# Two graph layers on one core: the products with W1 by Strassen's scheme on pairs of row tiles, and a first stage with B11 turned from PSUM and eleven slots for x

## The chip, the cores and the metric

The kernel runs on one core of one Trainium2 chip. The metric is the device time of one execution, in microseconds (us). Before the change it is 2218.14 us, the median of three runs (2216.73 to 2218.79). The profile is one execution of 2218.9 us.

## The reference, cut to what matters

`x` has 3327 rows of 512, `adj` is 3327 x 3327, all float32.

```python
h = relu(layernorm(x))
q, k, v = h @ Wq.T + bq, h @ Wk.T + bk, h @ Wv.T + bv
a = q @ k.T / sqrt(512) + adj + adj
x = x + softmax(a) @ v

h = relu(layernorm(x))
A2 = adj + eye
dscale = diagonal(A2) ** -0.5
temp = A2 @ h @ W1.T
x = x + relu((dscale[:, None] * A2 * dscale[None, :]) @ temp)
```

The product that is changed is the one with `W1.T`: the rows of `A2 @ h`, 26 tiles of 128 rows, each 128 x 512, times a 512 x 512 matrix, each row then scaled by `dscale`.

## The kernel before

**Stages.** A first stage (lines 269 to 377) merges Wq and Wk into one matrix M, normalizes and turns the 26 row tiles of x, and multiplies them with M. The score stage (lines 382 to 566) makes the exponentials of all scores. Then three large products follow one another, g = 0, 1, 2: the softmax weights times h, A2 times the new h, and A2 times temp. All are in float32, and all use Strassen's scheme in a form with seven products, twice nested in the large ones.

**The three large products.** `steps` (line 933) lists 294 steps: for each g, for each outer product r in `ORDER` (p5, p1, p6, p7, p2, p3, p4), for each of two column strips s (448 and 384 columns per matmul), the steps t = 0 to 5 and a short one, t None. A step loads its left tile three steps ahead and adds up its four block sums on VectorE two steps ahead (`sums`, `four_sums`, lines 171 to 175, 760 to 766). A full step is seven matmuls into seven PSUM banks (lines 779 and 780); a short one is four (line 772). At the end of t = 5, `Gather.first` (lines 804 to 812) takes the first four banks into SBUF, one copy on ScalarE and four operations on VectorE. After the short step, `Gather.rest` (lines 824 to 828) takes the other four and `Gather.settle` (lines 830 to 841) adds the result to the regions `ct` that need it. The right-hand block of a later step is built by `Right.make` (lines 737 to 749; lines 746 and 179 to 182 for p4), which is called three steps before the first strip's step t, so during the last steps of the strip before and the first ones of its own.

**Rows between the steps.** As soon as regions of `ct` are complete, their row tiles go through a 512 x 512 weight: Wv after g = 0 (`attend`), W1 after g = 1 (`temp`, lines 896 to 901), one tile after each full step from step (g = 1, p3, second strip, t = 2) on, into g = 2's p5. `times_weights` (lines 868 to 873) does four matmuls of 512 columns into one PSUM bank that the steps don't use; ScalarE scales the rows by `sd` (dscale) on the way out (line 900), and the tile is stored for g = 2.

**What sets the order.** The large products stand inside `in_order` (lines 122 to 136): each of the five engines runs its instructions in the order in which the program lists them. That order is `run(k)` (lines 1010 to 1037): the loads of step k + 3, the matmuls of step k, `rest` if the step is short, the sums of step k + 2, `first` if t = 5, `settle` if the step is short, then what is listed between the steps (`make`, loads, row tiles). The first stage stands outside `in_order`: there the framework orders each engine's queue. A tile framework inserts the waits between engines and keeps a buffer from being overwritten before its readers are done. `x_ring` (line 269) has seven buffers for x tiles. Lines 307 to 312 take M's blocks out of PSUM, form differences of them (`four_differences`, lines 177 to 182), and turn the sign of the first, B11, in place.

Of the kernel before, what the change touches and what calls it, by code (L numbers as in the profile page):

```python
# [10 lines left out]
F32 = mybir.dt.float32  # L11
AF = mybir.ActivationFunctionType
ALU = mybir.AluOpType
AX = mybir.AxisListType

P = 128
# [20 lines left out]
PAIRS = 6  # L37
# [6 lines left out]
ROW = tuple(STRIPS[s] + y * HT[s] + k for y in range(2) for s in range(2) for k in range(HT[s]))  # L44
# [3 lines left out]
def graph_layers_kernel(  # L48
# [28 lines left out]
    nc = tc.nc  # L77
    N = out.shape[0]
    NP, D = x.shape
    DC = D // P  # L80
    NT = NP // P
    scale = 1.0 / math.sqrt(D)
    E = D // 2
# [16 lines left out]
    def large(k, shape, name):  # L100
        return arena.tile(shape, F32, name=name, tag=f"large{k}")

    def mid(k, shape, name):
        return arena.tile(shape, F32, name=name, tag=f"mid{k}")

    def half(k, shape, name):
        return arena.tile(shape, F32, name=name, tag=f"half{k}")

    def bank(k, name):
        return banks.tile([P, BW], F32, name=name, tag=f"bank{k}")  # L110

    def ring(*slots):

        turn = itertools.cycle(slots)

        def take(shape, name):
            kind, k = next(turn)
            return kind(k, shape, name)

        return take  # L120
# [17 lines left out]
    const = ctx.enter_context(tc.tile_pool(name="const", bufs=1))  # L138
# [29 lines left out]
    rowd = [[dram.tile([P, D], F32, name=f"row{g}_{i}") for i in range(NT)] for g in range(3)]  # L168
# [5 lines left out]
        nc.vector.tensor_add(o[:, 2], o[:, 1], g[:, 0])  # L174
        nc.vector.tensor_add(o[:, 3], o[:, 2], g[:, 2])  # L175

    def four_differences(b):

        yield nc.vector.tensor_sub(b[4], b[0], b[1])
        yield nc.vector.tensor_add(b[5], b[3], b[4])  # L180
        yield nc.vector.tensor_sub(b[6], b[1], b[3])
        yield nc.vector.tensor_sub(b[7], b[2], b[5])
# [32 lines left out]
    B = {"m1": 0, "p2": 2, "p3": 3, "p5": 4, "p6": 5, "p7": 6, "p4": 7}  # L215
# [14 lines left out]
    class Chain:  # L230
# [7 lines left out]
        def __init__(self, product, first, more, last):  # L238


            X, Y, Z = x_bank("X"), y_bank("Y"), z_bank("Z")
            product(Y, "m1", True)
            first(0, Y, -1)
            product(Z, "p5", True)
            first(3, Z, -1)
            product(X, "p2", True)
            more(0, X)
            product(Y, "p6", False)
            first(1, Y, -1)
            Chain.finish()  # L250
            product(Z, "p3", False)
            more(1, Z)
            product(Y, "p7", False)
            more(3, Y)

            def rest():
                product(Y, "p4", False)
                first(2, Y, 1)
                last()

            Chain.before = rest
# [4 lines left out]
                Chain.before()  # L266
            Chain.before = None

    x_ring = ring(*((mid, k) for k in range(10, 15)), (half, 13), (half, 14))
    n_ring = ring(*((mid, k) for k in range(4)))  # L270

    def load_x(i, queue=nc.sync):
# [6 lines left out]
    def blocks(slots, name):  # L279

        return [b[:, k] for b in (half(j, [P, 2, 2, E], name) for j in slots) for k in range(2)]
# [3 lines left out]
    first = {}  # L285
# [7 lines left out]
    M = blocks(range(4, 8), "M")  # L293
# [8 lines left out]
    ps = [bank(k, "mm") for k in range(DC)]  # L302
    for c in range(DC):
        for r in range(DC):
            nc.tensor.matmul(ps[r], w_q[c // 2][:, c % 2, r * P : (r + 1) * P], w_k[c // 2][:, c % 2],
                             start=c == 0, stop=c == DC - 1)
    for r in range(DC):
        for z in range(2):
            nc.scalar.mul(M[2 * (r // 2) + z][:, r % 2], ps[r][:, z * E : (z + 1) * E], scale)
    for _ in four_differences(M):  # L310
        pass
    nc.scalar.mul(M[0], M[0], -1.0)

    def h_transposed(k):

# [53 lines left out]
    for r in range(DC):  # L369
        for c in range(DC):  # L370
            nc.tensor.matmul(pu[:, r : r + 1], w_k[c // 2][:, c % 2, r * P : (r + 1) * P], bq_sb[:, c : c + 1],
                             start=c == 0, stop=c == DC - 1)
# [144 lines left out]
    steps = [(n, t) for n in range(len(groups)) for t in range(HALF)]  # L517
# [32 lines left out]
    with in_order(*(e.engine for e in (nc.vector, nc.tensor, nc.gpsimd, nc.sync))):  # L550
# [9 lines left out]
        k = len(steps)  # L560
# [16 lines left out]
    ROLE = {"p1": 0, "p6": 2, "p7": 4, "p5": 6, "p2": 7, "p3": 1, "p4": 5, "p8": 3}  # L577
# [35 lines left out]
    sd = const.tile([P, NT], F32, name="sd")  # L613
    rs = const.tile([P, NT], F32, name="rs")

    def weights(src):

        w = [half(k, [P, 2, D], "w") for k in (12, 13)]
        for c in range(DC):
            nc.sync.dma_start(w[c // 2][:, c % 2], src[c * P : (c + 1) * P])  # L620
        return [w[c // 2][:, c % 2] for c in range(DC)]
# [14 lines left out]
    def prepared():  # L636
        nc.vector.reciprocal(rs, tot)
        nc.vector.tensor_scalar(dg, dg, 1.0, None, op0=ALU.add)
        nc.gpsimd.tensor_tensor(sd, dg, mh, op=ALU.pow)

    wv_w1 = []

    def other_weights():
        wv_w1.append(weights(w1T))


    parts = {}
# [1 line left out]
    def view(k, j):  # L649
        if k not in parts:  # L650
            n = PACKS[k][1]
            parts[k] = large(k, [P, n, 4, Q[0]], f"part{k}")
        return parts[k][:, j]
# [9 lines left out]
    cts = {}  # L663
# [9 lines left out]
    spare = [(mid, k) for k in range(10, 15)]  # L673
# [1 line left out]
    x_slots = [lambda k=k: view(2, 1).rearrange("p a w -> p (a w)")[:, k * D : (k + 1) * D] for k in range(3)]  # L675
    x_slots = itertools.cycle([*x_slots, lambda: mid(10, [P, D], "xt")])
    h_ring = ring((mid, 11))
    ts_ring = ring(*spare[:3])
    xr_ring = ring(*spare[:3], (half, 14))
    out_ring = ring((half, 12), (half, 13), *spare[3:])  # L680
    xr_last = ring(*((half, k) for k in (4, 5, 6)))
# [23 lines left out]
    class Right:  # L705
# [9 lines left out]
        def rows(self, dst, h, z):  # L715

            for k, i in enumerate(self.its):
                src = rowd[self.g][ROW[h * HALF + i]]
                nc.sync.dma_start(dst[:, k], src if z is None else src[:, z * E : (z + 1) * E])
# [31 lines left out]
    class Step:  # L751
# [8 lines left out]
        def sums(self):  # L760
            for a, d in self.diagonals:
                nc.vector.tensor_add(a, a, d)
            if self.t is None:
                return
            self.o = o_ring3()[:, :, : Q[self.s]]
            four_sums(self.o, self.a.rearrange("p k y w -> p (k y) w"))
# [76 lines left out]
    def where(i):  # L843

        s = int(i >= STRIPS[1])
        return (s, *divmod(i - STRIPS[s], HT[s]))
# [21 lines left out]
    def times_weights(i, w):  # L868
        s, y, k = where(i)
        ps = bank(ROLE["p8"], "p8")  # L870
        for d in range(DC):
            nc.tensor.matmul(ps, cts[s][y][d][:, k * P : (k + 1) * P], w[d], start=d == 0, stop=d == DC - 1)  # L872
        return ps
# [19 lines left out]

    normed = {}

    def temp(i):

        ps = times_weights(i, wv_w1[1])
        ts = ts_ring([P, D], "ts")
        nc.scalar.mul(ts, ps, sd[:, i : i + 1])  # L900
        nc.gpsimd.dma_start(rowd[2][i], ts)

    xrs = {}

# [28 lines left out]
    steps = [Step(g, r, s, t, rights[g, r, t]) for g in range(3) for r in ORDER for s in range(2) for t in every]  # L933
# [3 lines left out]
    def number_of(g, r, s, t):  # L937
        return ((g * len(ORDER) + r) * 2 + s) * len(every) + t

    def at(k, what, *args):  # L940
        between.setdefault(k, []).append((what, args))

    early = []
    for g in range(3):
        for n, r in enumerate(ORDER):
            for t, e in enumerate(every):
                k = number_of(g, n, 0, t)
# [9 lines left out]
    for n, job in enumerate(jobs):  # L957
        k = k0 + n * (k1 - k0) // len(jobs)
# [3 lines left out]
    def rows(g, k, i, *z):  # L962

        if g == 0:
            at(k - 2, attend_load, i)
            at(k, attend, i)
            at(k + 1, attended, i)
        elif g == 1:
            at(k, temp, i)
        else:  # L970
            at(k - 1, finish_load, i, *z)
            at(k, finish, i, *z)

    for g in range(2):
        k = number_of(g, 5, 1, 2)
        for i in ROW:
            if steps[k].t is None:
                k += 1  # L980
            rows(g, k, i)
            k += 1
    within = {}
    for (n, s, t), its in {
        (5, 1, 2): (0,), (5, 1, 3): (1,), (5, 1, 4): (2,), (5, 1, 5): (3,),
# [3 lines left out]
        for i, when in zip(its, (between, within)):  # L989
            if i is not None:  # L990
                k = number_of(2, n, s, t)
# [5 lines left out]
        at(number_of(2, 6, 1, 2) + n, last_load, i)  # L997
    for k, what in ((1, totals), (2, prepare), (6, prepared), (8, judge), (9, judged)):
        at(k, what)
    at(number_of(1, 1, 0, 4), other_weights)  # L1000

    for k in range(3):
        steps[k].load()
# [4 lines left out]
    banks_of, gathers = {}, {}  # L1008

    def run(k):  # L1010
        step = steps[k]
        if k + 3 < len(steps):
            steps[k + 3].load()
        if step.t == 0:
            banks_of.update(seven())
        if not cts:
            set_up()
        if step.t is None:
            banks_of["p8"] = bank(ROLE["p1"], "p8")
        t, sums = step.t, steps[k + 2].sums if k + 2 < len(steps) else tuple  # L1020
        if t == PAIRS - 1:
            gathers[step.r, step.s] = Gather(step.r, step.s, k == len(steps) - 2)
        gatherer = gathers.get((step.r, step.s))
        for j, _ in enumerate(step.multiply(banks_of)):
            if j == 3 and t == PAIRS - 1 and gatherer.last:
                gatherer.first(banks_of)
            for what, args in within.get(k, ()) if j == 3 else ():
                what(*args)
        if t is None:
            gatherer.rest(banks_of)  # L1030
        sums()
        if t == PAIRS - 1 and not gatherer.last:
            gatherer.first(banks_of)
        if t is None:
            gatherer.settle()
        for what, args in between.get(k, ()):
            what(*args)

    with in_order(*(e.engine for e in (nc.vector, nc.tensor, nc.gpsimd, nc.scalar, nc.sync))):
        for k in range(len(steps)):  # L1040
# [379 lines left out]
```

## Time and profile before

| | before |
|---|---|
| time, median of 3 | 2218.14 us |
| TensorE busy | 2181.7 us, 98% of the span |
| VectorE busy | 1628.5 us, 73% |
| ScalarE busy | 231.5 us, 10% |
| matmuls with Wv and W1 (L872) | 416 records of 512 columns, 123.5 and 65.7 us busy |

A row of the groups reads: line, engine, operation, output<-inputs by the program's names, shapes, count, then busy time and mean duration of one in ns, then the idle time of the engine before them and what ended it. A float32 matmul appears as two records. Durations of matmuls overlap, since they are pipelined; the distance between two starts is the time that one costs. In a list in order of time the columns are start, duration, engine, line, operation, and in brackets the idle time before it with its releaser. In a table of windows they are the window, its length, the busy time of PE, PEld (weight loads), DVE (VectorE), ACT (ScalarE) and POOL with counts, the mean granted clock of TensorE (1.00 is full), the busy share of the DMA engines, and GB/s. In several groups the name `part` stands for different views of the same large buffers, `ct` and the block sums `o` among them.

### The profile page before, as it was taken

To read this page: it belongs to the slowest core of one execution; us is meant where nothing else is said; L and a number is where in the kernel's file an instruction comes from. 1 tells how busy PE (TensorE), PEld (TensorE's weight loads), DVE (VectorE), ACT (ScalarE), POOL (GpSimd) and SP (SyncE) were. 2 spreads that over 40 slices of the span, in tenths; PEclk is the share of its full clock that TensorE was granted. 3 is DMA by queue.
4 is the path that set the end of the run, shared out by engine and by line. 5 is a ranking of instruction groups with operands and counts; after the bars stand their busy time and mean duration, and the time that the engine had idled before them with its cause. 6 is when DMAs were issued, how large, how long until landed. Compare 5 with 4: busy or idle time off the path is not lost.

```text
span 2218.9 us, 20976 instructions
## 1 busy us (share of the span) xinstructions
PE 2181.7 (98%) x6268; PEld 1169.2 (53%) x6268; DVE 1628.5 (73%) x3103; ACT 231.5 (10%) x336; POOL 356.1 (16%) x551
## 2 busy tenths in 40 slices
PE   9999999999999999999999999999999999999997
PEld 6555555455545555555454555555545555555554
DVE  6369888888877788787778778886645358777776
ACT  5312112112110000000001000000000000000011
POOL 4224333333331000001222100000000000000001
PEclk9999999999999999999999999999999999999999
DMA  7558888888969898888797899876645458765685
GB/s 252 211 206 296 292 304 281 301 286 309 348 198 322 310 371 309 273 297 298 261 314 258 303 340 355 283 277 199 225 142 179 135 188 294 248 194 183 206 303 171
DMA packets 246682, 583.68 MB, mean 263 GB/s; under 512 B 34768, under 2 KB 106270, under 8 KB 246558
## 3 DMA queue, kind: packets, MB, share of 16 engines
q1 hardware_dynamic: 192270, 399.28, 54.2%
q0 software_dynamic: 44928, 167.49, 19.9%
q10 hardware_dynamic: 9360, 15.47, 2.1%
q8 instruction: 52, 0.85, 0.2%
q14 instruction: 72, 0.59, 0.1%
HBM read 414.28 MB, written 167.85 MB: 262 GB/s over the span
## 4 chain that ended last, share of the span: by engine, by line
PE 81%; issue 6%; DMA 4%; DVE 4%; POOL 3%; ACT 0%; SPq 0%; POOLq 0%; ACTq 0%; DVEq 0%
PE p L780 52%; PE Y L452 9%; PE p L872 8%; PE p L772 5%; PE Z L452 4%; PE X L452 2%; DMA g<-in_adjT_dram 1%; DMA xt<-in_x_dram 1%; PE Y L345 1%; DVE part L173 1%; DMA xr<-x1d 1%; DMA p<-g 0%; POOL sum L444 0%; PE pt L925 0%; POOL p L460 0%
## 5 line engine op out<-in xcount | busy, mean ns | idle before, releaser
L780 PE MATMUL p<-part,b 128*128 128x448 f32 (+1 forms) x3528 | 1255.4, 514 | 6.1 <-DVE part L174 4.9
L780 PEld LDWEIGHTS p<-part,b 128*128 128x128 f32 x3528 | 669.2, 190 | 571.8 <-issue 309.9
L173 DVE TENSOR_TENSOR part<-part 128x896 f32<-128x896 f32 (+1 forms) x252 | 257.1, 1020 | 95.8 <-PE p L780 50.6
L452 PE MATMUL Y<-qt,hp 128*128 128x448 f32 (+1 forms) x832 | 311.1, 516 | 4.9 <-DVE g L456 3.8
L452 PEld LDWEIGHTS Y<-qt,hp 128*128 128x128 f32 x832 | 157.8, 191 | 142.2 <-issue 73.8
L452 PE MATMUL Z<-qt,hp 128*128 128x384 f32 (+1 forms) x416 | 162.5, 513 | 0.0
L175 DVE TENSOR_TENSOR part<-part,part 128x448 f32<-128x448 f32 (+1 forms) x219 | 129.5, 591 | 16.6 <-DVE part L174 0.5
L174 DVE TENSOR_TENSOR part<-part,part 128x448 f32<-128x448 f32 (+1 forms) x219 | 129.5, 591 | 7.4
L772 PE MATMUL p<-part,b 128*128 128x448 f32 (+1 forms) x336 | 124.2, 513 | 0.0
L872 PE MATMUL p<-w,ct 128*128 128x512 f32 x272 | 123.5, 593 | 0.5 <-DVE part L884 0.5
L452 PEld LDWEIGHTS Z<-qt,hp 128*128 128x128 f32 x416 | 78.8, 190 | 67.4 <-issue 37.2
L456 DVE SCALAR_TENSOR_TENSOR g<-g,Y 128x384 f32<-128x384 f32 (+1 forms) x156 | 91.4, 586 | 29.0 <-PE Y L452 26.3
L866 POOL DMA_DIRECT2D sum<-job x52 | 28.4, 547 | 504.1 <-DVE job L863 285.5
L809 DVE TENSOR_TENSOR part<-p,part 128x384 f32<-128x384 f32 (+1 forms) x33 | 19.4, 586 | 106.5 <-PE p L780 105.9
L772 PEld LDWEIGHTS p<-part,b 128*128 128x128 f32 x336 | 63.6, 190 | 53.7 <-issue 32.3
L808 ACT COPY part<-p 128x384 f32<-128x384 f32 (+1 forms) x33 | 16.6, 503 | 685.4 <-PE p L780 684.6
L872 PEld LDWEIGHTS p<-w,ct 128*128 128x128 f32 x272 | 51.5, 190 | 59.8 <-issue 51.9
L452 PE MATMUL X<-qt,hp 128*128 128x384 f32 (+1 forms) x208 | 81.1, 512 | 0.0
L459 ACT ACTIVATE g<-g 128x768 f32<-128x768 f32 (+1 forms) x48 | 43.0, 896 | 357.3 <-DVE g L456 293.1
L444 POOL DMA_DIRECT2D sum<-o x52 | 36.8, 709 | 224.9 <-DVE o L438 154.1
L872 PE MATMUL p<-w,part 128*128 128x512 f32 x144 | 65.7, 592 | 0.0
L92 POOL DMA_DIRECT2D out_dram<-r x30 | 16.2, 542 | 303.9 <-DVE r L928 268.8
(166 smaller groups left out, 1881.5 us busy)
## 6 DMA issues: line engine op xcount, KB each, us to landing
part<-sum SPq DMA_DIRECT2D x104, 448.0 KB, 5.0
part<-p SPq DMA_DIRECT2D x91, 448.0 KB, 6.5
part<-sum SPq DMA_DIRECT2D x104, 384.0 KB, 3.5
part<-p SPq DMA_DIRECT2D x91, 384.0 KB, 4.1
part<-in_adjT_dram SPq DMA_DIRECT2D x78, 448.0 KB, 4.6
b<-row SPq DMA_DIRECT2D x234, 128.0 KB, 4.9
part<-in_adjT_dram SPq DMA_DIRECT2D x78, 384.0 KB, 3.7
g<-in_adjT_dram SPq DMA_DIRECT2D x52, 448.0 KB, 4.5
```

What stands on the lines that cost most here:

```text
L173: nc.vector.tensor_add(o[:, 0:2], g[:, 0:4:3], g[:, 1:2].to_broadcast([P, 2, g.shape[-1]]))
L174: nc.vector.tensor_add(o[:, 2], o[:, 1], g[:, 0])
L175: nc.vector.tensor_add(o[:, 3], o[:, 2], g[:, 2])
L345: nc.tensor.matmul(ps[:, :w], M[B[name]][:, c, o * P : (o + 1) * P], hp[k][:, A[name], c], start=start and c == 0, stop=c == 1, skip_group ...
L444: nc.gpsimd.dma_start(self.to(sumd)[:, 0:2], self.o)
L452: nc.tensor.matmul(ps[:, :wd], h_of(self.t, name, k), qt[B[name]][:, k], start=start and k == 0, stop=k == 1, skip_group_check=True)
L456: nc.vector.scalar_tensor_tensor(a[n], a[n], 2.0, ps[:, :wd], op0=ALU.mult, op1=ALU.add if sign > 0 else ALU.subtract)
L459: nc.scalar.activation(g[1], g[1], AF.Exp, **({"bias": pad} if self.t == HALF - 1 else {}))
L772: yield nc.tensor.matmul(ps[("p2", "p3", "p4", "p8")[k]][:, :w], b[:, z], a[:, 0, y], start=k == 3, stop=True)
L780: yield nc.tensor.matmul(ps[r][:, :w], b[:, i], m, start=self.t == 0, stop=self.t == PAIRS - 1 and r in ("p1", "p5", "p6", "p7"))
L866: nc.gpsimd.dma_start(sumd[self.s][self.j][:, 2 + self.k], self.a)
L872: nc.tensor.matmul(ps, cts[s][y][d][:, k * P : (k + 1) * P], w[d], start=d == 0, stop=d == DC - 1)
```

## The change

**W1.** A pair of row tiles, each 128 x 512, is taken as a 2 x 2 block matrix: its blocks are the two halves of each tile along the 512 that is summed over. W1 is loaded as four blocks of 256 x 256, and four differences of them are formed ahead, in the second stage. One pair then takes seven products, each of two matmuls with 256 columns, in place of eight block products. VectorE forms four block sums of the pair's rows (eight additions of 128 x 128) at the end of the step before; the seven products are set among the matmuls of two steps, two matmuls apart. They share one PSUM bank, in two halves. Four products leave PSUM through ScalarE, three through VectorE, which adds them to what is there. The scaling by `sd`, or by its negative `nsd`, is done on the way. In these steps the sums of step k + 2 are listed after the second matmul, and not after the last.

**First stage.** M's first block leaves PSUM with its sign turned, and the first difference is formed from the turned block in one operation; the separate turning goes. Nine buffers of one kind and two of another hold x tiles, eleven in place of seven.

The diff, cut:

```diff
-    def four_differences(b):
-        yield nc.vector.tensor_sub(b[4], b[0], b[1])
+    def four_differences(b, first=0):
+        if first == 0:
+            yield nc.vector.tensor_sub(b[4], b[0], b[1])
...
-    x_ring = ring(*((mid, k) for k in range(10, 15)), (half, 13), (half, 14))
+    x_ring = ring(*((mid, k) for k in range(6, 15)), (half, 13), (half, 14))
...
-            nc.scalar.mul(M[2 * (r // 2) + z][:, r % 2], ps[r][:, z * E : (z + 1) * E], scale)
-    for _ in four_differences(M):
+            turned = -scale if r < 2 and z == 0 else scale
+            nc.scalar.mul(M[2 * (r // 2) + z][:, r % 2], ps[r][:, z * E : (z + 1) * E], turned)
+    nc.vector.scalar_tensor_tensor(M[4], M[0], -1.0, M[1], op0=ALU.mult, op1=ALU.subtract)
+    for _ in four_differences(M, 1):
         pass
-    nc.scalar.mul(M[0], M[0], -1.0)
...
+        nc.scalar.mul(nsd, sd, -1.0)
...
-    def temp(i):
-        ps = times_weights(i, wv_w1[1])
-        ts = ts_ring([P, D], "ts")
-        nc.scalar.mul(ts, ps, sd[:, i : i + 1])
-        nc.gpsimd.dma_start(rowd[2][i], ts)
+    PARTS = (("p2", 1, True, 0, 1), ("m1", 0, True, 0, -1), ("p5", 1, False, 3, -1), ("p6", 0, False, 1, -1),
+             ("p3", 1, False, 1, 1), ("p7", 0, False, 3, 1), ("p4", 0, False, 2, 1))
+    AFTER = ((0, 0), (0, 2), (0, 4), (0, 6), (1, 1), (1, 3), (1, 5))
+    class Temp:
...
+        def sums(self):
+            a11, a12, a21, a22 = self.blocks = [
+                [cts[s][y][2 * z + c][:, k * P : (k + 1) * P] for c in range(2)]
+                for s, y, k in map(where, self.its) for z in range(2)
+            ]
+            self.o = half(14, [P, 4, 2, P], "rows")
+            for k, x, y in ((1, a21, a22), (2, None, a11), (3, None, a12), (0, a11, a21)):
+                for c in range(2):
+                    nc.vector.tensor_add(self.o[:, k, c], self.o[:, {2: 1, 3: 2}[k], c] if x is None else x[c], y[c])
+        def product(self, j):
+            name, h, new, n, sign = PARTS[j]
+            if j == 0:
+                self.ps = bank(ROLE["p8"], "pw").rearrange("p (k e) -> p k e", k=2)
+                self.to = [next(ts_slots)() for _ in self.its]
+            left, ps = {"m1": 0, "p2": 1, "p4": 3}.get(name), self.ps[:, h]
+            for c in range(2):
+                a = self.o[:, {"p7": 0, "p5": 1, "p6": 2, "p3": 3}[name], c] if left is None else self.blocks[left][c]
+                nc.tensor.matmul(ps, a, W[B[name]][:, c], start=new and c == 0, stop=c == 1, skip_group_check=True)
+            i = self.its[n // 2]
+            to, by = self.to[n // 2][:, n % 2 * E : (n % 2 + 1) * E], (sd if sign > 0 else nsd)[:, i : i + 1]
+            if name in ("p2", "p5", "p6", "p4"):
+                nc.scalar.mul(to, ps, by)
+            else:
+                nc.vector.scalar_tensor_tensor(to, ps, by, to, op0=ALU.mult, op1=ALU.add)
+            if j == len(PARTS) - 1:
+                for i, ts in zip(self.its, self.to):
+                    nc.gpsimd.dma_start(rowd[2][i], ts)
...
+    k = number_of(1, 5, 1, 2)
+    for n in range(0, NT, 2):
+        if steps[k].t is None:
+            k += 1
+        w = Temp(*ROW[n : n + 2])
+        last_of[k - 1] = w.sums
+        for j, (later, m) in enumerate(AFTER):
+            inserted.setdefault((k + later, m), []).append((w, j))
+        k += 2
...
+        weighs = any((k, j) in inserted for j in range(7))
+        for j, _ in enumerate(itertools.chain((None,), step.multiply(banks_of))):
+            for w, n in inserted.get((k, j), ()):
+                w.product(n)
...
+            if weighs and j == 2:
+                sums()
         if t is None:
             gatherer.rest(banks_of)
-        sums()
+        if not weighs:
+            sums()
         if t == PAIRS - 1 and not gatherer.last:
             gatherer.first(banks_of)
         if t is None:
             gatherer.settle()
         for what, args in between.get(k, ()):
             what(*args)
+        if k in last_of:
+            last_of[k]()
```

## The prediction

> **What bounds the kernel now.** I read first the shares of busy time and the costliest groups.
>
> ```profile
> PE 2181.7 (98%) x6268; PEld 1169.2 (53%) x6268; DVE 1628.5 (73%) x3103; ACT 231.5 (10%) x336; POOL 356.1 (16%) x551
> ...
> L872 PE MATMUL p<-w,ct 128*128 128x512 f32 x272 | 123.5, 593 | 0.5 <-DVE part L884 0.5
> ```
>
> TensorE is the bound: 98% busy, so time leaves only with matmul columns or with its few idle microseconds, and each new wait of TensorE is paid in full. Next, the stage with the W1 products, as one window (PE, PEld, DVE, ACT, POOL, clock, DMA):
>
> ```profile
> 1560.00:1800.00 240.00, 240.00 (x646) 122.38 (x646) 113.03 (x215) 20.23 (x31) 14.03 (x26) 1.00 0.55 172
> ```
>
> Here TensorE never waits, and VectorE is busy 113 of 240 us. An average hides bursts, so I read the order of time across one change of strip, TensorE first:
>
> ```profile
> 1584.31 4.68 PE L780 MATMUL p<-part,b 128*128 128x384 f32 x14
> 1588.83 3.60 PE L872 MATMUL p<-w,ct 128*128 128x512 f32 x8
> 1592.26 2.74 PE L772 MATMUL p<-part,b 128*128 128x384 f32 x8
> 1594.84 5.42 PE L780 MATMUL p<-part,b 128*128 128x448 f32 x14
> ```
>
> That is step t = 5, a W1 tile, the short last step (t None), step t = 0 of the next strip. Each f32 matmul is two records. VectorE over the same change:
>
> ```profile
> 1585.87 0.56 DVE L809 TENSOR_TENSOR part<-p,part 128x384 f32<-128x384 f32 x1 [12.19 <-PE p L780]
> ...
> 1588.15 0.68 DVE L746 TENSOR_TENSOR b<-b,rows 128x512 f32<-128x512 f32 x1
> ...
> 1593.11 0.55 DVE L825 TENSOR_TENSOR part<-part,p 128x384 f32<-128x384 f32 x1 [3.21 <-PE p L772]
> ...
> 1595.51 0.28 DVE L762 TENSOR_TENSOR part<-part,ident 128x128 f32<-128x128 f32 x1
> 1595.83 1.09 DVE L173 TENSOR_TENSOR part<-part 128x896 f32<-128x896 f32 x1
> ...
> 1598.16 1.82 DVE L841 TENSOR_TENSOR part<-part,part 128x768 f32<-128x768 f32 x2
> 1599.89 0.69 DVE L746 TENSOR_TENSOR b<-b,rows 128x512 f32<-128x512 f32 x1
> ...
> 1601.35 0.28 DVE L182 TENSOR_TENSOR b<-b 128x128 f32<-128x128 f32 x1
> 1601.56 0.28 DVE L762 TENSOR_TENSOR part<-part,ident 128x128 f32<-128x128 f32 x1
> ```
>
> From the short step on, VectorE works without a pause until long after TensorE has begun the next strip. Today nothing on TensorE needs it at once. Its parts, by differences of starts: `first` 2.28 (1585.87 to 1588.15), `make` 1.66 to 1.67 (1599.89 to 1601.56), `rest` 2.40, a diagonal 0.32, the sums 2.33, `settle` 1.73.
>
> Last, what a TensorE wait of this length does to its clock (window rows, then the matmuls), and two places in the first stage:
>
> ```profile
> 610.00:612.00 2.00, 0.00 (x0) 0.00 (x0) 1.53 (x4) 0.00 (x0) 0.00 (x0) 1.00 0.97 303
> 612.00:614.00 2.00, 1.72 (x3) 1.11 (x4) 1.92 (x5) 0.43 (x1) 0.68 (x1) 0.59 0.92 317
> 614.00:616.00 2.00, 2.00 (x4) 0.96 (x4) 1.34 (x3) 1.15 (x2) 1.31 (x3) 0.56 0.66 245
> ```
> ```profile
> 612.28 4.54 PE L452 MATMUL Y<-qt,hp 128*128 128x384 f32 x8 [2.48 <-DVE g L456]
> 619.24 2.74 PE L452 MATMUL Y<-qt,hp 128*128 128x384 f32 x8
> ```
> ```profile
> 24.07 0.63 ACT L312 ACTIVATE M<-M 128x512 f32<-128x512 f32 x1 [5.53 <-DVE M L179]
> 62.00 0.63 PE L325 MATMUL tp<-ident,ht 128*128 128x128 f32 x4 [1.68 <-DVE hp L332]
> ```
>
> After 2.48 us of idleness the clock was about half, and eight records took 4.54 instead of 2.74: 1.8 us more.
>
> **What the Trainium skill says.** PSUM — Partial Sum Buffer, "PSUM bank collisions raise a hardware error": TensorE writing a bank while ScalarE or VectorE reads it is an error even in other columns. The new products share one bank in halves, so each must wait until the one before is read out, whichever half it used. No run before shows it; no bank is shared so. The same page, "The four PSUM rules": a starting matmul clears the written marks of the whole bank; so m1, started after p2, lets p5 overwrite p2's half. This fixes the order p2, m1, p5. TensorE: Matmul & The Clock Gate, "Architectural detail": VectorE and ScalarE queues are strict first-in first-out. The trace agrees: ScalarE stood 5.53 us at L312 while the two L309 copies behind it had their matmuls done. The same page, Part 1: about 3.4 us of idleness halve the clock and a busy window of 3.4 us restores it. The trace shows it after only 2.48 us, for about 3.7 us.
>
> **The change part by part.**
>
> *Columns.* A W1 tile now takes 3.43 us (1588.83 to 1592.26); 26 of them 89.2. Afterwards 13 pairs have 7 products of 2 matmuls, 28 records of 256 columns. No row has this width. Records of 384, 448 and 512 columns start 0.3225, 0.3762 and 0.429 us apart, all 0.84 ns per column, so 0.2145; the upper end is 0.22, from the transposes' 0.86 ns per column. The weight load hides: one-column matmuls of L371 start every 0.144 us (32 in 4.61). 13 x 28 x 0.2145 = 78.1. **Gain 11.1** (lower end 9.1).
>
> *New VectorE work.* Per pair eight 128x128 additions at 0.21 apart (L181 to L182), 0.28 the last: 1.76 us; and three evacuations 128x256 from PSUM, 0.41 by the like row L331 (bounds 0.33, its distance to the next, and 0.62, the 448-wide L456): 1.2. 13 x 3 = 39 us more in a window where VectorE has 127 idle; in the middle of a strip this lies beside matmuls. ScalarE's four 256-wide copies (0.36, by L330) for two of 0.69: hidden, it is 8% busy here.
>
> *The new waits.* p5 now stands in TensorE's queue behind m1's evacuation, and that stands in VectorE's queue behind the pair's eight additions, which stand behind everything of the strip change. `first` also moves late: its ScalarE copy follows p4's, which ends near the end of the t = 5 step (call it 0), so `first` starts at -0.14 (behind a 384-wide strip) or -0.3 (448). No W1 tile separates t = 5 from the short step any more. All later matmuls queue behind p5.
> - Pair at p4, first strip, t = 0: VectorE 2.28 + 1.66 + 2.40 + 0.32 + 2.33 + 1.73 + 1.67 + 1.76 + 0.41 = 14.56, done at 14.4. TensorE reaches p5 at 2.58 (short step) + 0.86 + 1.50 + 0.86 + 1.50 = 7.3. Wait 7.1, and 0.1 to pass the signal: **7.2**.
> - Third stage, p5, first strip: the same less the diagonal: **6.9**.
> - p4, second strip: `first` and `rest` 448 wide (2.28 and 2.40 times 625/558, by L174's two widths) 2.56 and 2.68, diagonal 0.32, sums 384 wide 2.13, settle 2.0 (two of L841 at 896 elements, 1084 ns less the overlap), no `make`, then 1.76 + 0.41 = 11.8, done at 11.5; TensorE, with matmuls of 0.752 at 448 and 0.645 at 384 columns, 3.01 + 0.86 + 1.29 + 0.86 + 1.29 = 7.3: **4.3**.
> - Third stage, second strip: no settle, no diagonal, 9.5, done at 9.2: **2.0**.
> - Elsewhere p4 waits for p7's evacuation behind the four sums: p7 ends, two matmuls of 0.645 follow, VectorE is 0.1 to 0.5 late, some four times: **1.1**.
> Together **21.5**. The first strip change before them holds no pair.
>
> *The clock.* Three of these waits are longer than 2.48 us; at 1.75 each **5.2**.
>
> *W1 blocks and signs.* Four VectorE differences of 0.68 in the second stage's p2 strip, at most one per step of 5.27 us, where sums and `make` leave room; one ScalarE sign and the negative of sd: 0, ScalarE is nearly idle.
>
> *First stage.* L312 is gone, and B11 leaves PSUM already turned, so ScalarE no longer stands 5.53 us. TensorE's idle 1.75 and 0.68 behind it should go, and with eleven x slots the waits for late tiles, 0.41 and 1.68. Of 4.5 I take **4.0**; ends 1 and 7, since the half clock from 22 to 32 us may also shorten. Nothing after it is slack: TensorE is busy on from 62.5.
>
> Sum: 2218.1 - 11.1 + 21.5 + 5.2 - 4.0 = **2229.7**.
>
> **Rivals.** (a) *The waits are hidden*: VectorE has half its time free. Against: the burst above sits exactly where the products come. Then -11.1 - 4.0: 2203. (b) *Products of different halves don't wait for each other*: p5 then waits only for its first block sum, 8 x 0.21 + 0.41 - 0.29 = 1.8 earlier at four places. 21.5 - 7.2 = 14.3; the clock falls twice, 3.5: 2220.8. For it: the addresses differ; against: the skill's bank rule. (c) *Deeper*: each fall of the clock lasts a second window (1.7 x 3), the evacuation costs 0.62, and the first stage gives 1: about 2239. For it: from 22 to 32 us the clock stayed at half for 10 us.
>
> **How the numbers follow.** Forecast 0.57, (a) 0.12, (b) 0.16, (c) 0.15. The forecast's spread, 2223 to 2236 (waits by 4, first stage by 3), is nearly all over 2222.6, where slower begins; (b) splits between same and slower. So faster 0.14, same 0.14, slower 0.72. The range 2216 to 2239 leaves out (a) and the top of (c).
>
> **What would show it.** Right: TensorE waits of 7, 4, 7 and 2 us at the t = 0 steps with pairs, put down to a VectorE evacuation or block sum; 364 records of 256 columns; a half clock after the long ones; no 5.5 us wait of ScalarE near 24 us. Wrong: a busy TensorE from 1560 to 1800, or a first stage that is ordered otherwise and gives or takes more than 4 us.

## The result and the profile after

The changed kernel takes 2225.25 us (median of six runs, 2222.34 to 2227.2) against 2216.14 us before (2214.74 to 2218.79). The ratio is 1.0039, with a 95% interval of 1.0026 to 1.0052: 8.6 us slower, between 5.8 and 11.5.

The two profiles shown differ less, 2220.3 against 2218.9 us. The profile of before is from a long run of that kernel, that of after from the shortest of its own. In the score stage and the first large product, which the change does not touch, the run of before has the 2.48 us wait with half clock that was shown, and one more half clock behind a 1.94 us wait. In the run of after no such wait of the score stage is that long, and behind the other one, 1.93 us there, the clock stayed full. So no difference of whole profiles is used below; stages are compared from one landmark to another.

The stage of the W1 products, from the start of step t = 0 in p3's second strip to the last short step of the strip in which the pairs end; the first row is the kernel before, the second the one after (columns as above):

```profile
1551.43:1796.29 244.86, 244.86 (x662) 125.40 (x661) 118.29 (x220) 20.23 (x31) 14.03 (x26) 1.00 0.55 171
```
```profile
1539.06:1797.32 258.26, 241.99 (x817) 157.40 (x816) 153.71 (x363) 26.67 (x57) 14.02 (x26) 0.97 0.50 162
```

The same steps take 258.26 us in place of 244.86: **13.4 us more**. TensorE, without a gap before, now stands idle for 16.3 us, and its clock is below full. VectorE has 35.4 us more work and is still idle for 105.

The waits, as TensorE's list over the whole run puts them down (who waited for whom, us in total, times, longest):

```profile
PE pw L953 <- DVE ts L959: 16.3, 5, 6.1
```

L953 is a product of a pair, L959 an evacuation by VectorE. TensorE at the strip change that was shown before (short step, p2, two matmuls, m1, two matmuls, then p5):

```profile
1578.95 2.74 PE L794 MATMUL p<-part,b 128*128 128x384 f32 x8
1581.53 1.03 PE L953 MATMUL pw<-w,ct 128*128 128x256 f32 x4
...
1584.76 1.67 PE L802 MATMUL p<-part,b 128*128 128x448 f32 x4
1592.55 2.08 PE L953 MATMUL pw<-w,rows 128*128 128x256 f32 x4 [6.12 <-DVE ts L959]
1594.41 2.26 PE L802 MATMUL p<-part,b 128*128 128x448 f32 x4
1596.51 1.03 PE L953 MATMUL pw<-w,rows 128*128 128x256 f32 x4
```

VectorE meanwhile, in the order first, make, rest, a diagonal, sums, settle, make, block additions, evacuation of m1, without a gap between them:

```profile
1578.73 0.56 DVE L831 TENSOR_TENSOR part<-p,part 128x384 f32<-128x384 f32 x1 [2.10 <-ACT part L830]
...
1580.85 0.68 DVE L768 TENSOR_TENSOR b<-b,rows 128x512 f32<-128x512 f32 x1
...
1582.50 0.55 DVE L847 TENSOR_TENSOR part<-part,p 128x384 f32<-128x384 f32 x1
...
1584.36 0.28 DVE L784 TENSOR_TENSOR part<-part,ident 128x128 f32<-128x128 f32 x1
1584.68 1.09 DVE L173 TENSOR_TENSOR part<-part 128x896 f32<-128x896 f32 x1
...
1587.00 1.82 DVE L863 TENSOR_TENSOR part<-part,part 128x768 f32<-128x768 f32 x2
1588.74 0.69 DVE L768 TENSOR_TENSOR b<-b,rows 128x512 f32<-128x512 f32 x1
...
1590.40 0.48 DVE L943 TENSOR_TENSOR rows<-ct,ct 128x128 f32<-128x128 f32 x2
...
1592.02 0.47 DVE L959 SCALAR_TENSOR_TENSOR ts<-pw,nsd,ts 128x256 f32<-128x256 f32 x1
```

VectorE works without a pause from 1578.73 to 1592.49, where m1's evacuation ends, and p5 starts 0.06 us later. TensorE had been ready at 1584.76 + 1.50 = 1586.26 (four records of 448 columns take 1.50). The clock behind it, as windows:

```profile
1588.00:1592.00 4.00, 0.00 (x0) 0.00 (x0) 3.93 (x14) 0.00 (x0) 0.00 (x0) 0.60 0.25 84
1592.00:1594.00 2.00, 1.46 (x4) 1.19 (x5) 1.93 (x5) 0.00 (x0) 0.00 (x0) 0.50 0.00 0
1594.00:1596.00 2.00, 2.00 (x5) 1.19 (x4) 1.93 (x4) 0.47 (x1) 0.00 (x0) 0.60 0.00 0
1596.00:1598.00 2.00, 2.00 (x8) 1.33 (x7) 0.76 (x4) 0.43 (x1) 0.00 (x0) 1.00 0.00 0
```

Four records of p5 take 1.86 us (1592.55 to 1594.41) in place of 0.86, the next four 2.10 (1594.41 to 1596.51) in place of 1.50: 1.6 us more at half clock.

The first stage, after; ScalarE, then TensorE:

```profile
18.81 0.66 ACT L311 ACTIVATE M<-mm 128x256 f32<-128x256 f32 x2 [0.20 <-PE mm L306]
19.36 0.59 ACT L330 COPY hp<-tp 128x512 f32<-128x512 f32 x1
```
```profile
23.83 1.09 PE L327 MATMUL tp<-ident,ht 128*128 128x128 f32 x4
...
96.03 2.31 PE L347 MATMUL Y<-hp,M 128*128 128x512 f32 x5 [0.72 <-ACT qs L352]
```

The copies that stood behind L312 until 25.14 now start at 19.36, and the matmuls that start at 23.83 started at 25.78 before, after a wait of 1.75 us. Those that start at 96.03 started at 101.09 before: 5.1 us gained.

### The profile page after: what moved, and what is told of

It reads as the page before. It is cut to its first block, busy times and chain, and to the rows that moved or that the text cites. A ratio compares the mean times of both kernels' runs of the same rounds, so it can differ in the third digit from the quotient of the medians.

```text
span 2220.3 us, 21475 instructions
## 1 busy us (share of the span) xinstructions
PE 2174.1 (98%) x6424; PEld 1200.5 (54%) x6424; DVE 1664.4 (75%) x3250; ACT 238.3 (11%) x363; POOL 357.4 (16%) x551
## 4 chain that ended last, share of the span: by engine, by line
PE 92%; DVE 5%; issue 1%; DMA 1%; ACT 0%; POOL 0%; SPq 0%; POOLq 0%; DVEq 0%; ACTq 0%
PE p L802 52%; PE Y L454 13%; PE Z L454 6%; PE p L794 4%; PE p L894 4%; PE pw L953 3%; PE X L454 3%; PE Y L347 2%; PE Z L347 1%; DVE part L173 1%; PE mm L306 1%; PE tp L327 1%; PE X L347 0%; DVE part L174 0%; PE pt L986 0%
## 5 line engine op out<-in xcount | busy, mean ns | idle before, releaser
L953 PE MATMUL pw<-w,rows 128*128 128x256 f32 x208 | 56.5, 396 | 15.8 <-DVE ts L959 15.8
L894 PE MATMUL p<-w,ct 128*128 128x512 f32 x136 | 61.8, 594 | 0.4 <-DVE part L906 0.4
L953 PEld LDWEIGHTS pw<-w,rows 128*128 128x128 f32 x208 | 40.9, 198 | 37.3 <-DVE ts L959 18.5
```

The costliest lines, as they stand in the source:

```text
L953: nc.tensor.matmul(ps, a, W[B[name]][:, c], start=new and c == 0, stop=c == 1, skip_group_check=True)
```

## The experiments

Times are medians; the ratio is to the kernel before on the same chip, with its 95% interval. It is formed from all the runs, so it is not quite the ratio of the two medians; the differences in us follow the ratio.

**The first stage alone.** The kernel before, with

```diff
-    x_ring = ring(*((mid, k) for k in range(10, 15)), (half, 13), (half, 14))
+    x_ring = ring(*((mid, k) for k in range(6, 15)), (half, 13), (half, 14))
...
-            nc.scalar.mul(M[2 * (r // 2) + z][:, r % 2], ps[r][:, z * E : (z + 1) * E], scale)
+            turned = -scale if r < 2 and z == 0 else scale
+            nc.scalar.mul(M[2 * (r // 2) + z][:, r % 2], ps[r][:, z * E : (z + 1) * E], turned)
...
-    nc.scalar.mul(M[0], M[0], -1.0)
```

and the first difference formed from the turned block.

> The kernel before with the first stage's edits alone (B11 turned as it leaves PSUM, eleven slots for x); W1 as before. Theory (the two parts add up): 5.1 us faster than before, as the first stage is shorter by that in the profile after; the chain that ended last no longer has ScalarE's 5.5 us wait near 24 us. Rival (an earlier first stage only makes the score stage wait longer for its transfers): within 1.5 us of before.

Measured: 2211.39 against 2218.24 us, ratio 0.9971 (0.9961 to 0.9981): 6.4 us faster. The gain reaches the end of the run; the rival is out.

**W1 alone.** The changed kernel, with the edit above taken back.

> The changed kernel with the first stage of before; the W1 products are the new ones. Theory: 13 to 14.5 us slower than before: 11.1 us of matmul columns less, 17 us of TensorE waits for the evacuation of m1 (6.3, 3.2, 6.0, 1.0 and 0.6), 6 us of half clock behind the three long ones. Rival (the waits in the changed kernel come from the earlier first stage or from transfers that it moved): 11 us faster or about as before.

Measured: 2231.42 us, ratio 1.0057 (1.0043 to 1.0071): 12.6 us slower (9.5 to 15.7). The waits are 6.14, 3.07, 5.81, 0.86 and 0.44 us, as in the changed kernel:

```profile
PE pw L952 <- DVE ts L958: 16.3, 5, 6.1
```

They belong to the W1 products. The two parts add up to 6.2 us slower; the whole was 8.6, and the intervals overlap.

**Block additions early.**

```diff
             gatherer.rest(banks_of)
+            if k in last_of:
+                last_of[k]()
...
-        if k in last_of:
+        if k in last_of and t is not None:
             last_of[k]()
```

> The changed kernel; at the end of a strip the eight block additions of the next pair come right after the short step's evacuations, ahead of the four sums, settle and make; m1's evacuation stays where it was. Theory (p5 waits for m1's evacuation, which shares its PSUM bank, and that stands behind everything in VectorE's queue): the same time as the changed kernel within 2 us, the waits 6.3, 3.2, 6.0 and 1.0 us unchanged within 0.3, put down to the evacuation. Rival (p5 waits for its block sum alone): the four waits shrink to under 1 us and the time falls by 15 to 22 us.

Measured: 2227.66 us, ratio 1.0042 (1.0026 to 1.0057), the waits the same to 0.02 us. VectorE's two additions for p5 and its evacuation of m1, then TensorE's p5:

```profile
1586.80 0.49 DVE L943 TENSOR_TENSOR rows<-ct,ct 128x128 f32<-128x128 f32 x2
...
1594.46 0.48 DVE L959 SCALAR_TENSOR_TENSOR ts<-pw,nsd,ts 128x256 f32<-128x256 f32 x1
```
```profile
1594.99 2.08 PE L953 MATMUL pw<-w,rows 128*128 128x256 f32 x4 [6.14 <-DVE ts L959]
```

p5's block sum is there at 1587.29. p5 starts only after m1's evacuation has ended at 1594.94, although m1 lies in the bank's other half. So it is the evacuation that holds it. The wait is one that the tile framework put into the program. Why it must wait for the other half is not shown by a run: the reason that the prediction gave is the Trainium skill's rule (PSUM — Partial Sum Buffer, "PSUM bank collisions raise a hardware error") that TensorE must not write a bank which VectorE is reading, even in other columns. A run with m1 in a bank of its own was not tried: the kernel uses banks 0 to 7, seven for the steps and one for the pair.

**Settle late.**

```diff
         if t is None:
-            gatherer.settle()
+            if k in last_of:
+                late.append(gatherer.settle)
+            else:
+                gatherer.settle()
...
                 w.product(n)
+            if late and j == 2:
+                late.pop()()
```

> The changed kernel; at the end of a strip with a pair behind it, settle comes after m1's evacuation in the next step, and not before the block additions. Theory (each microsecond of VectorE work taken from in front of m1's evacuation shortens the wait by as much): the waits fall from 6.3, 3.2, 6.0, 1.0 to 4.5, 1.2, 4.2, 1.0; the clock no longer falls after the second; 6 to 8 us faster than the changed kernel. Rival (VectorE's queue is not what p5 waits for, its data or the bank come late for another reason): the time of the changed kernel within 1.5 us.

Measured: 2218.43 us, ratio 1.0006 (0.9995 to 1.0017), so some 7.3 us less than the changed kernel (the difference of the two ratios). Three of the waits, and what follows the second:

```profile
1593.37 2.08 PE L953 MATMUL pw<-w,rows 128*128 128x256 f32 x4 [4.39 <-DVE ts L959]
...
1648.60 1.13 PE L953 MATMUL pw<-w,rows 128*128 128x256 f32 x4 [1.07 <-DVE ts L959]
1649.57 1.45 PE L802 MATMUL p<-part,b 128*128 128x384 f32 x4
...
1701.71 1.67 PE L953 MATMUL pw<-w,rows 128*128 128x256 f32 x4 [4.07 <-DVE ts L959]
```

They fell by 1.73, 1.99 and 1.73 us. In the profile of the changed kernel settle takes 1.74, 2.01 and 1.73 us at these places, from its start to the next one. The 1.45 after the second is full clock. The rival, the time of the changed kernel within 1.5 us, is out.

**First early.**

```diff
+        soon = t == PAIRS - 1 and (gatherer.last or weighs)
...
-            if j == 4 and t == PAIRS - 1 and gatherer.last:
+            if j == 4 and soon:
                 gatherer.first(banks_of)
...
-        if t == PAIRS - 1 and not gatherer.last:
+        if t == PAIRS - 1 and not soon:
```

> The changed kernel; in the steps t = 5 with a pair, the first four banks are taken out after the fourth matmul, ahead of p4, and not at the end of the step. Theory (the late start of first is one of the terms of the wait): VectorE comes to rest before the short step's matmuls are done, so the waits fall from 6.1 and 5.8 to about 3.9 and 3.6 at the first strips; at the second strips rest is held by the matmuls anyway, so 3.1 and 0.9 become about 2.7 and 0.5; 5 to 7 us faster than the changed kernel. Rival (first's place costs nothing, since rest would have to wait for the short step): waits as in the changed kernel within 0.4 us, time within 1.5 us.

Measured: 2218.15 us, ratio 1.0006 (0.9997 to 1.0016): again some 7.3 us less. The waits are 3.97, 2.68, 3.64 and 0.47 us, each within 0.1 of what was expected, so the late start of `first` was one of the terms.

**m1 by ScalarE**, on top of the early block additions.

```diff
+            if name == "p3":
+                c11 = self.to[0][:, 0:E]
+                nc.vector.tensor_add(c11, c11, m1_out())
+            if name == "m1":
+                nc.scalar.mul(m1_out(), ps, by)
-            if name in ("p2", "p5", "p6", "p4"):
+            elif name in ("p2", "p5", "p6", "p4"):
                 nc.scalar.mul(to, ps, by)
```

> The changed kernel with the block additions early, and with m1 taken out of PSUM by ScalarE into a buffer of its own, from which VectorE adds it later, ahead of p3's evacuation (one addition of 128x256 more in each pair). Nothing is left out. Theory (p5 waited for VectorE only because m1's evacuation stood in its queue): the waits at p5 go, under 0.3 us each; but p3's evacuation now meets the same unbroken work, so p7 waits at the first strips, 2 to 4 us each; in all 4 to 8 us of waits in place of 16.3, and 8 to 14 us faster than the changed kernel. Rival (p5 is held by VectorE for its block sums or for other data): p5 waits as before.

Measured: 2213.86 us against 2217.17, ratio 0.9987 (0.9980 to 0.9993): 2.9 us faster than before, and so some 11.5 less than the changed kernel, as expected. No wait at p5 is left; two at p7 have come:

```profile
1606.36 2.07 PE L956 MATMUL pw<-w,rows 128*128 128x256 f32 x4 [3.67 <-DVE ts L967]
...
1713.47 1.35 PE L956 MATMUL pw<-w,rows 128*128 128x256 f32 x4 [3.01 <-DVE ts L967]
```

The unbroken work is the same; it now meets p3's evacuation. This is a version faster than before, but the first stage's gain alone is larger.

**The burst reordered.** VectorE's work at a strip change in another order, nothing left out:

```diff
+            if late and j == 2:
+                late.pop()()
+            if second and t != PAIRS - 1 and j == 4:
+                while later:
+                    later.pop()()
+                sums()
-            if j == 4 and t == PAIRS - 1 and gatherer.last:
+            if j == 4 and t == PAIRS - 1 and (gatherer.last or weighs):
                 gatherer.first(banks_of)
...
+        if opens:
+            last_of[k]()
+            late.append(sums)
...
+        if opens:
+            later.append(gatherer.settle)
```

`opens` is a short step with a pair behind it, `second` the second step of a pair; `make` joins `later` too.

> The changed kernel with VectorE's work at a change of strip listed otherwise: the first four banks are taken out after the fourth matmul of t = 5; after rest come the pair's block additions at once; the sums of step k + 2 follow m1's evacuation, make and settle follow p7's in the step after; in the second step of a pair the sums follow p7's evacuation. Nothing is left out. Theory (the waits are the only loss of the W1 part): TensorE waits under 1 us in all at the W1 products, no fall of the clock there, 20 to 24 us faster than the changed kernel, 14 to 17 faster than before. Rival (VectorE is short of time in this stage, so that a burst that is moved gives its wait back in the next step): waits of 5 us or more in all, put down to block sums or to later evacuations, and no faster than the kernel with the first stage alone.

Measured: 2206.98 us against 2217.61, ratio 0.9946 (0.9932 to 0.9960): 12 us faster than before, where 14 to 17 were expected. Neither forecast was quite right: of 17 us of waits 3.5 are left, 1.69 and 1.36 us in new places, at p5 of the second pair of a strip, and the 0.44 at p4 that was there before. The two new ones:

```profile
PE pw L953 <- DVE part L959: 3.0, 2, 1.7
```

**The burst reordered again**, the run before with settle moved into a gap:

```diff
+            if second and later and j == 2:
+                later.pop(0)()
```

> The reordered kernel, with settle moved once more: into the 1.6 us that VectorE stands idle ahead of p7's evacuation, and not behind it. In the reordered kernel TensorE still waited 1.69 and 1.36 us, at p5 of the second pair of a strip: the moved work had come to stand before that pair's m1. Theory (the length of VectorE's unbroken work ahead of m1 sets the wait): these two waits go, 0.5 us is left in all; 2.5 to 3.5 us faster than the reordered kernel, about 15 faster than the kernel before. Rival (the work is only moved to the next place again): waits of 1 us or more elsewhere at the W1 products, the time of the reordered kernel within 1.5 us.

Measured: 2201.16 us against 2217.17, ratio 0.9928 (0.9916 to 0.9941): **16 us faster than before**, the fastest of all. The waits of TensorE from 1490 to 1830 us, all of them:

```profile
PE pw L953 <- DVE ts L959: 0.4, 1, 0.4
```

The stage now takes 235.3 us (1539.69 to 1775.01), 9.5 less than before, of the 10.8 that the columns save. So the columns saved are real, and nearly all of the loss lay in the waits and the clock behind them. It is some 4 us faster than the run before it (the intervals, 13.1 to 18.6 and 8.9 to 15.1 us, leave that difference open by several us); 2.5 to 3.5 were expected.

**The two edits of the first stage, each alone.** In the one, the turn and seven slots; in the other, the slots and the old turn.

> The kernel before with B11 turned as it leaves PSUM; seven slots for x as before. Theory (each part of the first stage removes its own idle time): 2 to 3.5 us faster than before; TensorE's 1.75 us near 25 us is gone, the 1.68 us near 60 us stays. Rival (the wait of ScalarE is only moved to the next late tile of x): within 1 us of before.

> The kernel before with eleven slots for x; B11 turned by a second pass as before. Theory: 1.5 to 3 us faster than before; the 1.68 us near 60 us is gone, ScalarE's wait of about 5.5 us near 24 us stays. Rival (the slots do nothing for a stage that is held up by ScalarE's queue): within 1 us of before.

Measured: 2215.38 against 2217.61 us, ratio 0.9989 (0.9981 to 0.9997), 2.4 us faster; and 2214.08, ratio 0.9984 (0.9977 to 0.9990), 3.5 us faster, a little more than the 1.5 to 3 expected. Each part gives something alone. With the turn alone the 1.75 us wait is gone and the 1.68 us wait stays (now at 59.08 us). With the slots alone it goes, though a wait of 1.58 us has come (at 35.43 us) and that of 0.41 has grown to 0.68 (at 57.02 us), and ScalarE still waits, but 4.16 us and not 5.5: the difference that ScalarE waits for also starts earlier (L179 at 22.44 us, 23.36 before), as VectorE no longer stands 1.47 us for an x tile just ahead of it. There the expectation, that this wait would stay, was wrong.

## Why the prediction was right

The prediction was 2229.7 us, slower, from four terms.

| term | predicted | measured |
|---|---|---|
| columns | -11.1 | -10.8 |
| waits | +21.5 | +17.1, and 0.8 in small ones |
| clock | +5.2 | +6.1 |
| first stage | -4.0 | -6.4 |
| in all | +11.6 | +8.6 |

The last row is the measured difference of the whole, and not the sum of the rows above it.

*Columns.* Four records of 256 columns start 0.862 us apart, 0.2155 each for the 0.2145 taken; 364 of them 78.4, against 89.2.

*Waits.* The mechanism was as described: p5 behind m1's evacuation behind the burst, and at the four places named. From start to start they are 6.3, 3.2, 6.0 and 1.0 us, for 7.2, 4.3, 6.9 and 2.0; 0.6 at p4, and some 0.1 each at further ones. All were taken about 1 us too long, since I read VectorE's parts from a trace in which it waited within them. In the old trace rest runs beside the short step's matmuls, one result after another: 2.40 us. Coming late it finds all of them done and takes 1.86 (1582.50 to 1584.36). First took 2.12 for 2.28, the additions 1.62 for 1.76. These three make 0.84 of the 0.9 by which VectorE was done earlier (13.5 after the t = 5 step, not 14.4). At p4's second strip it is the same: rest took 2.13 (1641.27 to 1643.40) for 2.68. TensorE's side, 7.3 us to p5, was exact.

*Rivals.* (b) falls with the early block additions: p5's data were there 7.7 us before it started. (a) held in one respect only: VectorE has time enough in this stage, as the last reordering shows, but not at that moment. (c) held in one point: after the third long wait the half clock cost 2.7 us. Its other terms did not come: the evacuation took about 0.4 us from its start to the next one, not 0.62, and the first stage gave more than 1 us.

*Clock.* It fell three times, as said: 1.6, 1.8 and 2.7 us lost. That it fell behind the second of the waits, 3.06 us long, was in part luck. The prediction took one fall behind 2.48 us for a rule, and other traces of this case have full clock behind waits of 2.68 and 3.09 us (see the last section).

*First stage.* Larger than the 4.0 taken, within the ends named (1 and 7). In the profile it is 5.1. Of these, 3.7 us are idle time of TensorE (3.21 us up to 96.03, 6.90 up to 101.09 before). The waits of 1.75 and 1.68 us are gone, but the 0.68 that the prediction counted too is still there, and 0.41 has become 0.67. The other 1.4 us are busy time, as the half clock before 32 us also ended earlier. One of the signs of being wrong that the prediction named did come here: the stage gave more than 4 us, and it is ordered otherwise. Much of VectorE's queue and three matmuls on TensorE stand in other places. How much of the gain is due to that order no run separates.

Together the measured terms give 6.8; the measured difference of 8.6 has an interval of 5.8 to 11.5, and the stages by landmark give 13.4 - 5.1 = 8.3. The prediction was 3 us too slow: its waits were too long and its first stage's gain too small, and the clock term, too low by 0.9, made up for a part.

## What to carry to other kernels

An engine's average says nothing of an order that must be kept: VectorE was idle for 40% of the stage, and the wait came from 13.3 us of work listed ahead of one 0.5 us evacuation. Before putting an evacuation on an engine, add up what that engine has been told to do first, from the point where it last waited. And moving such work can bring the wait back at the next place in the queue, as two of the runs here show, so it belongs in the gaps, with the matrix engine's due times beside it.

## What the runs showed of the hardware that I had not expected

The length of a wait does not by itself decide whether the clock falls. All twelve profiles of this case have a wait of 1.93 or 1.94 us near 880 us, in the first large product, which no edit touches. Behind it the clock fell to half in five of them (the kernel before is one) and stayed full in seven (the changed kernel is one). It also stayed full behind 2.68 us in the run with `first` early and behind 3.09 us near 610 us in the run with m1 by ScalarE, but fell behind waits of 3.01 to 3.07 us in four traces, that one among them. It fell behind every wait of 3.64 us or more, eleven in all. The lost time differed too, 1.6 to 2.7 us for one fall in the changed kernel. So a single fall in one trace gives neither a limit nor a price. And the same four evacuations by VectorE take 0.65 us each (start to start) while the matmuls that fill their banks run just ahead of them, and 0.47 when these are done.
